# Slot projections: norm factors spread over the channels through DRAM instead of TensorE, and the order of the first loads

## The chip, the cores and the metric

The kernel runs on one core of one Trainium2 chip. The metric is device time in microseconds (us) of that core; the runs of the kernel before gave 1819.5, 1820.17 and 1820.96, median 1820.17. The engines are named as in the profile: PE (TensorE matmul; PEld its weight loads), DVE (VectorE), ACT (ScalarE), POOL (GpSimd), SP (SyncE, here only a queue that issues DMAs). PSUM is the accumulator memory that PE writes, SBUF the 128-partition on-chip memory.

## The reference

x is a float32 picture of 512 x 512 points (i, j) with 64 channels. Two layers add to it:

```
x = x + L0(gn(x))         # gn: normalize over the picture, per pair of channels (32 groups)
x = x + L1(gn(x))
```

L0 normalizes each point over its 64 channels, `xn = ln(gn(x))`, and makes two gated projections, masked by a vector m of 512 zeros and ones:

```
left  = (xn @ left_w  + left_b)  * m_i m_j * sigmoid(xn @ lgate_w + lgate_b)
right = (xn @ right_w + right_b) * m_i m_j * sigmoid(xn @ rgate_w + rgate_b)
out   = ln(einsum('kjd,kid->ijd', left, right)) @ out_w + out_b
L0    = out * sigmoid(xn @ ogate_w + ogate_b)
```

L1 keeps the first 12 x 12 Fourier modes of the picture, mixes their channels with complex weights and transforms back. All arithmetic is float32.

## The kernel before, in words

Only points whose row and column both have mask 1 give anything to the einsum. So the kernel first ranks the 512 positions (those with mask 1 first) and, if at most 256 have mask 1, works on 256 "slots" (K = 256) in place of 512 positions. The trace shows this path, `compact`.

*Ranks (lines 59 to 132).* The mask and a few constant tables are loaded by DMA; four loads of the mask, then few_i, c_tri, c_ones, c_iota and c_table go out on SP's queue, c_ident, c_center and the other constants on ACT's. DVE casts the mask into c_table (L95), two matmuls count (cum_ps), and DVE makes rank_p. Then hot, a 512 x 512 table of zeros and ones that says which position has which rank, is made by four DVE instructions of 128x512 (L116). For each of four blocks of 128 ranks four matmuls (L120) turn it into slot_t, and DVE makes src_i from it, the list of addresses for the gathers (L126). slot_row is the same as a row, read into registers by ACT and POOL.

*Gathers (lines 640 to 700).* For each of 16 column chunks jc, POOL issues four indirect DMAs of 1 MB (L632), which fetch x's rows in the order of the ranks. PE transposes the tiles, DVE takes statistics for the group norm (L681, L682), ACT copies 22 and POOL 10 of the chunk's columns to the slots of xc (L667), in turn. xc holds 128 partitions x 257 slots x 2 halves r x 64 channels: half r, partition p is the row of rank r*128+p. At the end `group_norm_affine` makes ab1, the scale and shift per channel, by a chain of small DVE instructions with two matmuls (mean_ps, var_ps).

*Slot projections (lines 703 to 789): the place of the change.* The 256 column slots are taken in 64 groups q of four. The loop's order is written out by hand (`manual_schedule`): each engine runs its instructions in the order of the program, and iteration q works on several groups at once. For one group, in order of its stages:

- `channels`: four transposes (xc_ps) put 2 x 64 channels on the partitions and 512 points on the free axis; ACT applies the affine of the group norm and writes gc_t, one of 12 buffers.
- `centered`: four matmuls with the centring matrix (cc_ps), ACT squares (sqc), DVE sums over the channels (L781) into total, 8 numbers per partition and group; here points are on the partitions again.
- `factors`: for QB = 4 groups together nine small DVE steps make 1/sqrt(variance) (rq_out, 128x32). The steps wait in a list, three of which run in each iteration.
- `spread`: POOL copies the 8 factors of a group over 64 channels each (rbc, L736).
- `normed`: four transposes by PE bring them to the layout of gc_t (rc_ps, L742), and DVE multiplies (xnc, L744).
- `project`: two matmuls each for gates and sides (L750), ACT's sigmoid (sigc, one buffer), two DVE instructions (bias added, times sigmoid: o_c, two buffers), two stores of 256 KB on SP's queue to left_d and right_d.

The loop starts 10 iterations before the first group is projected (`range(-QB - 6, groups)`). xc_ps has two PSUM buffers, cc_ps, rc_ps, gates and sides one each.

*After that* come the 64 products of the einsum (left_raw, right_raw loaded, L835 to L857), output norm, gate, statistics and the forward transform in one long pipeline, and the last layer with the stores of the result. The change does not touch these.

Of the kernel before, what the change touches and what calls it, by code (L numbers as in the profile page):

```python
# [17 lines left out]
P = 128  # L18
N = 512
# [27 lines left out]
def conv_preact_kernel(ctx: ExitStack, tc: tile.TileContext, t: dict):  # L47
# [11 lines left out]
    for b in range(4):  # L59
        nc.sync.dma_start(mask_i32[:, b : b + 1], t["sequence_mask"][:, b * P : (b + 1) * P].rearrange("o p -> p o"))  # L60

    def load_const(name, shape):
        c = const.tile(shape, F32, name=name)
        nc.scalar.dma_start(c, t[name])
        return c

    ident = load_const("c_ident", [P, P])
    center = load_const("c_center", [P, P])
    avg_p = load_const("c_avg_p", [P, P])
    avg_c = load_const("c_avg_c", [P, P])  # L70
    avg_h = load_const("c_avg_h", [P, 2])
    pick = load_const("c_pick", [P, G])
# [7 lines left out]
    nc.sync.dma_start(few_i, t["c_iota"][:, : NJ // 2])  # L80
    n_i = const.tile([1, 1], I32, name="n_i")
    with tc.tile_pool(name="ix", bufs=1) as xp, tc.tile_pool(
# [3 lines left out]
        def load_here(name, shape):  # L86
            c = xp.tile(shape, F32, name=name)
            nc.sync.dma_start(c, t[name])
            return c

        tri = load_here("c_tri", [P, P])
        ones = load_here("c_ones", [P, P])
        iota = load_here("c_iota", [P, N])
        table = load_here("c_table", [P, 4, 2 + M2])
# [20 lines left out]
        for b in range(4):  # L115
            nc.vector.tensor_scalar(hot[:, b, :], iota, rank_p[:, b : b + 1], None, ALU.is_equal)  # L116
        for sb in range(4):
            slot_ps = xps.tile([P, 2 + M2], F32, name="slot_ps", bufs=2)
            for b in range(4):
                nc.tensor.matmul(  # L120
                    slot_ps, hot[:, b, sb * P : (sb + 1) * P], table[:, b, :], start=(b == 0), stop=(b == 3)
                )
            nc.vector.tensor_copy(slot_t[:, sb], slot_ps)
            base = xp.tile([P, 1], F32, name="base", bufs=2)
            nc.vector.tensor_scalar(base, slot_t[:, sb, 0:1], float(NJ), None, ALU.mult)
            nc.vector.tensor_scalar(src_i[:, sb, :], iota[:, :NJ], base, None, ALU.add)  # L126
# [489 lines left out]
    def compact(fc):  # L616
# [31 lines left out]
        with tc.tile_pool(name="xc", bufs=1) as cp:  # L648
            xc = cp.tile([P, K + 1, 2, C], F32, name="xc")
            with tc.tile_pool(name="f1", bufs=1) as sp, tc.tile_pool(name="f1x", bufs=2) as xp, tc.tile_pool(  # L650
# [43 lines left out]
                ab1 = group_norm_affine(fc, sets, 2 * stats.shape[2], "xc")  # L694


            with tc.tile_pool(name="fb", bufs=QB + 8) as gp, tc.tile_pool(name="fw", bufs=2) as wk, tc.tile_pool(
# [7 lines left out]
                gts, totals, rss, rbs, xns, todo = {}, {}, {}, {}, {}, []  # L705

                def channels(q):
                    tps = pt.tile([P, 4, P], F32, name="xc_ps")
                    for i in range(4):
                        nc.tensor.transpose(tps[:, i, :], xc[:, 4 * q + i].rearrange("p r c -> p (r c)"), ident)  # L710
                    gts[q] = gp.tile([P, N], F32, name="gc_t")
                    nc.scalar.activation(
                        gts[q], tps.rearrange("p i k -> p (i k)"), AF.Identity, bias=ab1[:, 1:2], scale=ab1[:, 0:1]
                    )

                def centered(q):
                    cps = pc.tile([P, 8, C], F32, name="cc_ps")
                    for i in range(4):
                        nc.tensor.matmul(
                            cps[:, 2 * i : 2 * i + 2, :], gts[q][:, i * P : (i + 1) * P], center, start=True, stop=True  # L720
                        )
# [7 lines left out]
                def factors(k):  # L729
                    rss[k], steps = rsqrt_steps(rp, totals.pop(k), 1.0 / C, EPS, [P, QB * 8])  # L730
                    todo.extend(steps)

                def spread(q):
                    k, n = divmod(q, QB)
                    rbs[q] = rp.tile([P, 8, C], F32, name="rbc")
                    nc.gpsimd.tensor_copy(rbs[q], rss[k][:, 8 * n : 8 * n + 8].unsqueeze(2).to_broadcast([P, 8, C]))  # L736

                def normed(q):
                    rps = pc.tile([P, N], F32, name="rc_ps")
                    flat = rbs.pop(q).rearrange("p (i r) c -> p i (r c)", r=2)  # L740
                    for i in range(4):
                        nc.tensor.transpose(rps[:, i * P : (i + 1) * P], flat[:, i, :], ident)  # L742
                    xns[q] = wk.tile([P, N], F32, name="xnc")
                    nc.vector.tensor_mul(xns[q], gts.pop(q), rps)  # L744
# [9 lines left out]
                for q in range(-QB - 6, groups):  # L754
# [10 lines left out]
                    if live(2):  # L765
                        spread(q + 2)
                    if live(QB + 6):
                        channels(q + QB + 6)
                    if live(QB + 5):
                        sq, total = centered(q + QB + 5)  # L770
# [9 lines left out]
                    if live(QB + 5):  # L780
                        nc.vector.tensor_reduce(total, sq, AX.X, ALU.add)  # L781
                        if (q + QB + 5) % QB == QB - 1:
                            factors((q + QB + 5) // QB)
# [674 lines left out]
```

## Time and profile before

| | us |
|---|---|
| median of the runs | 1820.17 (1819.5 to 1820.96) |
| the profiled execution | 1827.94 |
| its span | 1826.1 |
| PE busy | 1643.6 (90%) |
| DVE busy | 1422.8 (78%) |
| ACT busy | 961.5 (53%) |
| POOL busy | 945.0 (52%) |

Stages by their first and last instructions in the trace: first gather issued at 14.24; last statistics of the gathers done at about 202; first gates of the slot projections at 227.24; last store of left_d issued at 466.24; first load of left_raw at 469.54.

How to read the lines. A timeline line is start, busy time, engine, source line, operation, output<-inputs, shapes, count; in brackets how long the engine idled before and what ended that. SPq and ACTq are DMA issues on these queues. Several instructions of one kind that follow each other stand in one line (a float32 matmul counts as two). PEclk is the share of full clock that PE was granted. DMA share is the mean busy share of the core's 16 DMA engines.

### The profile page before, as it was taken

How to read it: one execution, taken by the hardware profiler on the slowest of the kernel's cores; microseconds unless marked ns; L12 is line 12 of the kernel's file. 1: busy time of each engine (PE TensorE's matmuls, PEld its weight loads, DVE VectorE, ACT ScalarE, POOL GpSimd, SP SyncE). 2: the span in 40 equal slices, each digit the busy share in tenths (PEclk: the TensorE clock that was granted, in tenths of full speed). 3: DMA queues.
4: the chain of work that ended last, by engine and by line, in shares of the span. 5: the costliest groups of instructions: out<-in, count | busy, mean ns of one | idle time of the engine just before them, and what ended most of it. 6: DMA issues, size and time to landing. Idle time of an engine off the chain costs nothing. (4 is left out here: it accounts for less than half of the span.)

```text
span 1826.1 us, 33612 instructions
## 1 busy us (share of the span) xinstructions
PE 1643.6 (90%) x11414; PEld 1290.0 (71%) x11414; DVE 1422.8 (78%) x2968; ACT 961.5 (53%) x1708; POOL 945.0 (52%) x711
## 2 busy tenths in 40 slices
PE   6779899999899999998999999999999967998772
PEld 5666666665687878897888888888888844665431
DVE  6989777777555547888999999999999996765542
ACT  3565565554222249986777777777777751111000
POOL 3656211111000005788999999999999892211120
PEclk9989899999899999999999999999999986555555
DMA  6999245555655512576866776777668689999999
GB/s 253 386 385 370 102 124 137 137 138 149 203 184 175 183 58 117 197 275 237 274 238 243 258 254 229 252 268 271 241 228 291 218 251 414 423 427 426 427 427 382
DMA packets 189573, 467.94 MB, mean 256 GB/s; under 512 B 34896, under 2 KB 134224, under 8 KB 148432
## 3 DMA queue, kind: packets, MB, share of 16 engines
q1 hardware_dynamic: 158496, 262.21, 42.4%
q0 software_dynamic: 27712, 201.40, 28.7%
q10 hardware_dynamic: 3184, 2.08, 0.4%
q8 instruction: 93, 1.52, 0.3%
q14 instruction: 88, 0.72, 0.1%
HBM read 278.05 MB, written 187.56 MB: 255 GB/s over the span
## 5 line engine op out<-in xcount | busy, mean ns | idle before, releaser
L982 PE MATMUL w_ps<-gate_x,xt_c 128*128 128x128 f32 x2048 | 280.6, 281 | 30.3 <-DVE z_t L1198 24.8
L1045 POOL TENSOR_TENSOR places<-places,z_t 128x1024 f32<-128x1024 f32 x127 | 301.0, 2370 | 8.0
L982 PEld LDWEIGHTS w_ps<-gate_x,xt_c 128*128 128x128 f32 x2048 | 252.5, 194 | 45.5 <-DVE z_t L1198 40.5
L982 PE MATMUL c_ps<-center_x,xt_c 128*128 128x128 f32 x2048 | 277.4, 279 | 1.3 <-ACT xt_c L1011 0.7
L982 PEld LDWEIGHTS c_ps<-center_x,xt_c 128*128 128x128 f32 x2048 | 253.6, 195 | 4.0 <-ACT xt_c L977 2.1
L1364 PE MATMUL l_ps<-places,rinv 24*128 24x512 f32 x512 | 207.8, 1125 | 28.5 <-DVE places L1371 18.5
L1100 DVE BATCH_NORM_STATS2 stats2c<-places 128x6 f32<-128x128 f32 x1024 | 220.6, 279 | 8.0 <-POOL places L1045 8.0
L1015 DVE TENSOR_REDUCE scratch<-sq_c 128x16 f32<-128x1024 f32 x160 | 194.6, 1216 | 29.6 <-ACT sq_c L1010 18.6
L1202 POOL TENSOR_TENSOR z_t<-z_t,bias_row_out 128x1024 f32<-128x1024 f32 x32 | 75.6, 2364 | 248.5 <-DVE z_t L1198 244.4
L1149 ACT ACTIVATE z_t<-z_t 128x1024 f32<-128x1024 f32 x128 | 135.4, 1058 | 129.1 <-DVE z_t L1204 111.5
L972 PE MATMUL t_ps<-c_ident,places 128*128 128x128 f32 x1280 | 200.4, 280 | 1.3 <-DVE places L857 1.3
L1364 PEld LDWEIGHTS l_ps<-places,rinv 24*128 24x128 f32 x512 | 120.5, 303 | 110.9 <-DVE places L1371 57.2
L972 PEld LDWEIGHTS t_ps<-c_ident,places 128*128 128x128 f32 x1280 | 145.7, 142 | 61.6 <-issue 53.9
L977 ACT ACTIVATE xt_c<-t_ps,ab_xc 128x512 f32<-128x512 f32 x256 | 176.0, 688 | 14.7 <-PE t_ps L972 13.6
L1198 DVE TENSOR_TENSOR z_t<-w_ps,rs_n 128x512 f32<-128x512 f32 x256 | 172.1, 672 | 9.8 <-PE w_ps L982 9.7
L1007 ACT ACTIVATE sq_c<-c_ps 128x512 f32<-128x512 f32 x256 | 150.5, 588 | 32.8 <-PE c_ps L982 31.3
L682 DVE BATCH_NORM_STATS2 stats1c<-x_ps 128x6 f32<-128x512 f32 x256 | 156.1, 683 | 11.7 <-PE x_ps L681 11.2
L1204 DVE TENSOR_TENSOR z_t<-z_t,scratch 128x1024 f32<-128x1024 f32 x128 | 156.3, 1221 | 9.9 <-ACT rs_n L1021 3.7
L1041 POOL TENSOR_TENSOR z_t<-z_t,places 128x1024 f32<-128x1024 f32 x64 | 151.5, 2367 | 14.7 <-ACT z_t L1149 14.6
L1041 POOL TENSOR_TENSOR z_t<-z_t,bias_row_out 128x1024 f32<-128x1024 f32 x63 | 149.2, 2368 | 5.7 <-ACT z_t L1149 5.4
L1371 DVE TENSOR_TENSOR places<-places,l_ps 128x512 f32<-128x512 f32 x176 | 109.5, 683 | 54.7 <-DMA places<-x_h,dst_i 43.6
L736 POOL COPY rbc<-rq_out 128x512 f32<-128x512 f32 x64 | 38.3, 613 | 212.4 <-DVE rq_out L209 132.0
(211 smaller groups left out, 2749.1 us busy)
## 6 DMA issues: line engine op xcount, KB each, us to landing
x_h<-places SPq DMA_DIRECT2D x64, 1024.0 KB
out_x<-places SPq DMA_DIRECT2D x44, 1024.0 KB
places<-u_d SPq DMA_DIRECT2D x512, 64.0 KB
out_x<-lx_t SPq DMA_DIRECT2D x20, 1024.0 KB
left_d<-o_c SPq DMA_DIRECT2D x64, 256.0 KB
right_d<-o_c SPq DMA_DIRECT2D x64, 256.0 KB
left_raw<-left_d SPq DMA_DIRECT2D x64, 256.0 KB
right_raw<-right_d SPq DMA_DIRECT2D x64, 256.0 KB
```

The source lines that it names most:

```text
L682: nc.vector.bn_stats(stats[:, 0, 16 * (jc % quarter) + 4 * r + c, :], ps.rearrange("p i k -> p (i k)"))
L972: nc.tensor.transpose(tps[:, i, :], flat[:, o : o + P], ident)
L977: nc.scalar.activation(xts[s], tps, AF.Identity, bias=ab1[:, 2:3])
L982: nc.tensor.matmul(ps[:, 2 * i : 2 * i + 2, :], xts[s][:, i, :], w, start=True, stop=True)
L1007: nc.scalar.activation(sq, cps, AF.Square)
L1015: nc.vector.tensor_reduce(totals[k % 2][:, 8 * (n - 1) : 8 * (n + 1)], sqs.pop(s // 2), AX.X, ALU.add)
L1041: nc.gpsimd.tensor_mul(zs[k, c], zs[k, c], u)
L1045: nc.gpsimd.tensor_add(xr, xr, zs.pop((k, c)))
L1100: nc.vector.bn_stats(st[k // 4][:, g, k % 4, :], x_of(k)[:, :, 2 * g : 2 * g + 2])
L1198: nc.vector.tensor_mul(z[:, 8 * odd : 8 * odd + 8, :], wps, rs)
L1204: nc.vector.tensor_add(z, z, bias_ps["ogate"].unsqueeze(1).to_broadcast([P, 16, C]))
L1364: nc.tensor.matmul(ps.rearrange("p j o -> p (j o)"), rinv[h, b, :], it[h], start=True, stop=True, tile_position=(32 * g, 0),)
```

## The change

Four edits, all with the same arithmetic:

1. *First loads.* The mask is one DMA in place of four. c_table and c_ones move to the front of ACT's queue, ahead of c_ident and the other constants; c_tri and c_iota follow the mask on SP, few_i comes after them.
2. *Marks.* hot is made in pieces of 128 ranks: the four pieces that block 0 needs, then those of block sb+1 after the matmuls of block sb.
3. *`at_work`.* Four matmuls of 128x512 after the last transposes of the gathers and one after var_ps, whose results nobody reads.
4. *Factors.* `spread` and `normed` change. For four groups together PE transposes rq_out once (to 32 x 128), ACT copies it out of PSUM, POOL's queue writes it to a DRAM tile rs_d (16 KB), and two more DMAs on POOL's queue, one for each half r, read it back to 64 partitions each, every partition reading the same four rows of 512 numbers: rbc is 128 x 4 x 512, two buffers. DVE multiplies from rbc directly. POOL's copies and PE's four transposes per group are gone. gc_t has no buffers of its own: `channels` writes over the group's part of xc, which it has just transposed. The loop starts 14 iterations ahead (lead = QB + 9), spread comes five iterations before the group's first multiply, and total's order of columns is (r, i) in place of (i, r).

```
-    for b in range(4):
-        nc.sync.dma_start(mask_i32[:, b : b + 1], t["sequence_mask"][:, b * P : (b + 1) * P].rearrange("o p -> p o"))
+    nc.sync.dma_start(mask_i32, t["sequence_mask"].rearrange("o (b p) -> p (o b)", p=P))
...
-        tri = load_here("c_tri", [P, P])
-        ones = load_here("c_ones", [P, P])
-        iota = load_here("c_iota", [P, N])
-        table = load_here("c_table", [P, 4, 2 + M2])
+        table = load_here(nc.scalar, "c_table", [P, 4, 2 + M2])
+        tri = load_here(nc.sync, "c_tri", [P, P])
+        ones = load_here(nc.scalar, "c_ones", [P, P])
+        iota = load_here(nc.sync, "c_iota", [P, N])
+        ident = load_const("c_ident", [P, P])
...
+        nc.sync.dma_start(few_i, t["c_iota"][:, : NJ // 2])
...
-        for b in range(4):
-            nc.vector.tensor_scalar(hot[:, b, :], iota, rank_p[:, b : b + 1], None, ALU.is_equal)
+        def mark(sb):
+            for b in range(4):
+                one = slice(sb * P, (sb + 1) * P)
+                nc.vector.tensor_scalar(hot[:, b, one], iota[:, one], rank_p[:, b : b + 1], None, ALU.is_equal)
+
+        mark(0)
         for sb in range(4):
...
+            if sb < 3:
+                mark(sb + 1)
...
+                def at_work(count):
+                    ps = pt.tile([P, 4, P], F32, name="x_ps")
+                    for _ in range(count):
+                        nc.tensor.matmul(ps, ident, flat[:, : 4 * P], start=True, stop=True)
+
+                at_work(4)
+                ab1 = group_norm_affine(fc, sets, 2 * stats.shape[2], "xc", with_variance=lambda ab: at_work(1))
...
+            rs_d = dram.tile([K // 4, 2, 4 * P], F32, name="rs_d")
...
+                def gts(q):
+                    return xc[:, 4 * q : 4 * q + 4].rearrange("p i r c -> p (i r c)")
...
-                def spread(q):
-                    k, n = divmod(q, QB)
-                    rbs[q] = rp.tile([P, 8, C], F32, name="rbc")
-                    nc.gpsimd.tensor_copy(rbs[q], rss[k][:, 8 * n : 8 * n + 8].unsqueeze(2).to_broadcast([P, 8, C]))
+                def spread(k):
+                    ps = pc.tile([QB * 8, P], F32, name="rc_ps")
+                    nc.tensor.transpose(ps, rss.pop(k), ident)
+                    turned = np_.tile([QB * 8, P], F32, name="turned_c")
+                    nc.scalar.copy(turned, ps)
+                    groups_d = rs_d[k * QB : (k + 1) * QB]
+                    nc.gpsimd.dma_start(groups_d.rearrange("n r (i p) -> (n r i) p", p=P), turned)
+                    rbs[k] = np_.tile([P, QB, N], F32, name="rbc")
+                    for r in range(2):
+                        h = slice(r * C, (r + 1) * C)
+                        nc.gpsimd.dma_start(rbs[k][h], groups_d[:, r].unsqueeze(0).to_broadcast([C, QB, N]))
...
                 def normed(q):
-                    rps = pc.tile([P, N], F32, name="rc_ps")
-                    flat = rbs.pop(q).rearrange("p (i r) c -> p i (r c)", r=2)
-                    for i in range(4):
-                        nc.tensor.transpose(rps[:, i * P : (i + 1) * P], flat[:, i, :], ident)
+                    k, n = divmod(q, QB)
                     xns[q] = wk.tile([P, N], F32, name="xnc")
-                    nc.vector.tensor_mul(xns[q], gts.pop(q), rps)
+                    nc.vector.tensor_mul(xns[q], gts(q), rbs[k][:, n])
...
-                for q in range(-QB - 6, groups):
+                lead = QB + 9
+                for q in range(-lead - 1, groups):
...
-                    if live(2):
-                        spread(q + 2)
-                    if live(QB + 6):
-                        channels(q + QB + 6)
-                    if live(QB + 5):
-                        sq, total = centered(q + QB + 5)
+                    if live(lead + 1):
+                        channels(q + lead + 1)
+                    if live(lead - QB) and (q + lead - QB) % QB == QB - 1:
+                        spread((q + lead - QB) // QB)
+                    if live(lead):
+                        sq, total = centered(q + lead)
```

In the changed program the order on each engine follows: on DVE the multiply of group q+1 comes first in iteration q, then up to three rsqrt steps, then o_c of group q and the reduce of group q+13; on PE gates(q), xc_ps(q+14), every fourth time the new transpose, cc_ps(q+13), sides(q).

## The prediction

> **What bounds the kernel now.** I read the page's slices first (which stage leans on what), then a table by stretches of 50 us, then one period of the slot projections in the timeline, then the two ends of the stretch that the change touches: the first 14 us and 199 to 215 us.
>
> ```profile
> PE   6779899999899999998999999999999967998772
> ...
> PEclk9989899999899999999999999999999986555555
> DMA  6999245555655512576866776777668689999999
> ```
>
> Slices are 45.7 us. The first four (gathers) are at 9 in DMA. Slices 5 to 10 are the slot projections: PE at 8 and 9, DMA at 4 and 5.
>
> ```profile
> core 0: us, PE busy (x) PEld busy (x) DVE busy (x) ACT busy (x) POOL busy (x), PEclk, DMA share, GB/s
> 100.00:150.00 50.00, 40.60 (x279) 34.05 (x280) 42.84 (x83) 28.16 (x95) 30.25 (x65) 0.90 0.97 381
> ...
> 300.00:350.00 50.00, 50.00 (x314) 32.29 (x312) 38.53 (x82) 29.68 (x40) 7.80 (x13) 1.00 0.55 138
> ```
>
> In the projections PE is busy 50.00 of 50 us at full clock, DVE 77%, ACT 59%. So there a TensorE instruction taken away is time, until the next engine is full. One period:
>
> ```profile
> 268.55 1.13 PE L750 MATMUL sides_c<-xnc,w_sides 64*128 64x512 f32 x4
> ...
> 269.51 1.02 PE L750 MATMUL gates_c<-xnc,w_gates 64*128 64x512 f32 x4
> ...
> 269.78 1.41 DVE L776 SCALAR_TENSOR_TENSOR o_c<-sides_c,b_sides,sigc 128x512 f32<-128x512 f32 x2 [1.23 <-ACT sqc L723]
> ...
> 270.47 0.65 PE L742 MATMUL rc_ps<-c_ident,rbc 128*128 128x128 f32 x4
> ...
> 270.96 0.60 PE L710 MATMUL xc_ps<-c_ident,xc 128*128 128x128 f32 x4
> ...
> 271.11 0.68 DVE L781 TENSOR_REDUCE total<-sqc 128x8 f32<-128x512 f32 x1
> ...
> 271.31 1.11 ACT L759 ACTIVATE sigc<-gates_c,b_gates 128x1024 f32<-128x1024 f32 x1 [1.55 <-DVE o_c L776]
> ...
> 271.40 1.06 PE L719 MATMUL cc_ps<-c_center,gc_t 128*128 128x128 f32 x8
> ...
> 271.70 0.68 DVE L744 TENSOR_TENSOR xnc<-gc_t,rc_ps 128x512 f32<-128x512 f32 x1
> ...
> 272.32 0.77 ACT L712 ACTIVATE gc_t<-xc_ps,ab_xc 128x512 f32<-128x512 f32 x1
> ```
>
> The next sides start at 272.38: 3.83 us a period, and from start to start PE's five blocks take 0.96, 0.96, 0.49 (rc_ps), 0.44 and 0.98, without a gap.
>
> ```profile
> 4.94 0.43 SPq L88 DMA_DIRECT2D c_table<-in_c_table  x1
> 7.63 0.17 DVE L95 CAST c_table<-mask_i 128x4 f32<-128x4 int32 x1 [7.63 <-DMA c_table<-in_c_table]
> ...
> 10.82 1.68 DVE L116 TENSOR_SCALAR hot<-c_iota,rank_p 128x512 f32<-128x512 f32 x4
> ...
> 11.36 6.90 PEld L120 LDWEIGHTS slot_ps<-c_table,hot 128*128 128x128 f32 x32 [2.37 <-DVE hot L116]
> ...
> 14.24 1.08 POOL L632 DMA_INDIRECT xg<-in_x,src_i  x1 [13.78 <-DVE src_i L126]
> ```
>
> The stretches after the gathers, in the columns of the table above:
>
> ```profile
> 199.21:203.94 4.73, 0.00 (x1) 0.01 (x1) 4.53 (x12) 0.00 (x0) 2.83 (x10) 1.00 0.00 0
> 203.94:209.34 5.40, 2.98 (x13) 2.50 (x13) 3.00 (x19) 0.83 (x2) 0.00 (x0) 0.50 0.00 0
> 209.34:214.86 5.52, 5.34 (x25) 4.88 (x25) 0.71 (x2) 2.64 (x5) 0.00 (x0) 0.56 0.00 0
> ```
>
> The first gather waits for a chain that starts with c_table, the last of nine issues on SP. After the gathers PE idles 4.7 us and then runs at clock 0.50 until about 214.
>
> The profiled execution took 1827.94 us (span 1826.1), 7.8 above the median 1820.17; I sum against it and move the difference to the median.
>
> **The change, part by part.**
>
> **Ranks' chain.** c_table goes to the front of ACT's queue (issued at 0.75 as c_ident was), and the mask is one transfer at 0.76 in place of four. By c_table's own 2.69 us from issue to use (4.94 to 7.63) the table is there at 3.4. The mask moves 512 scattered elements in one transfer; I give it half a microsecond more, so the CAST starts at about 4.2 instead of 7.63: 3.4 us. c_tri (second on SP, 1.2+2.7=3.9) and c_iota (1.7+2.7=4.4, needed 3.2 after the CAST) don't end later. The first marks are 128 wide: four at 0.42 pitch become four at 0.17 (the small DVE rows of this chain) to 0.42, but the four matmuls behind them keep 0.44 each (7.03/16), so only about 0.3 is gained. The later marks sit on DVE before a slot's copy, 0.7 us of work within the 1.7 us that PE needs for a slot. Sum -3.7; from -4.6 (mask as quick as the table) to 0 (mask as late as the table was). The other constants and few_i, moved behind these, are needed after 20 us. The whole gather stage behind it moves along: its copies alternate ACT and POOL without a break and its DMA share is 0.97 wherever it starts.
>
> **at_work.** Four matmuls of 512 columns at 0.48 (half of the 0.96) fill PE from 199.2 to about 201.1, one more follows var_ps, before transposes that wait for ab anyway (done 207.95, used 208.51: 0.56 us of cover for 0.5 to 1.0). If PE then stays at full clock, the first two iterations from 209.34 take 2 x 1.85 (the later pitch, 214.86, 216.70, 218.55) instead of 5.52: -1.8; if not, 0 to +0.4. The row shows only that 4.7 us of idling ends at clock 0.50; the longest gap left is 2.8. I take -1.8, since 2.8 is well short of 4.7; by the row alone it could be either. The Trainium skill, "TensorE: Matmul & The Clock Gate" (The HAM clock gate), says the clock is halved after an idle window of about 3.4 us; by it a gap of 2.8 us leaves the clock up, -1.8, and one of 4.7 us does not.
>
> **Longer lead.** The loop starts 14 iterations ahead instead of 10: 4 x 1.85 = +7.4 before the first gates, while PE does nothing else. The same channel work ends four iterations earlier at the end: four iterations fall from 3.83 to the bare pitch of the tail (2.79, from 452.43, 455.21, 458.00): -4.2.
>
> **Factors.** Out of PE: four transposes, 0.49 a period. In: one transpose of a 32-column piece per four groups, 0.12/4=0.03. Period 3.37; x50 iterations with all the work: 50 x 0.46 = -23.0. Covered beside it: DVE (0.68+0.68+1.41 and three short steps at 0.21; start to start 3.16, under 3.37), with the multiply now reading SBUF twice, for which I keep 0.68 and bound 0.59 to 0.75; ACT (1.11+0.77+0.60, and 0.3 of copy in one of four). POOL loses its copies (0.61) and gets three DMA issues per four groups; nothing else waits on POOL in this stage. gc_t is now written into xc itself, with PE and ACT waiting only as they did.
>
> **DMA.** Stores move 134 GB/s at share 0.53, so 253 GB/s when full, 2.0 us of all engines per period. Per four groups come 16 KB written and two loads of 512 KB. At 393 GB/s (gathers, 381/0.97) the loads cost 2.7 us, at the stores' 253 (also 64 partitions at a time) 4.1; the worst row of this trace, the first loads (100 GB/s at 0.60, 4 to 6 us), makes 6.3. I take 4.1: 8.1+4.1=12.2 of 13.5 us, share 0.9.
>
> **The new wait.** The multiply of a fourth group waits for the loads; behind it on DVE stand the rsqrt steps, o_c and the reduce, and PE's gates wait for it. spread's copy ends about 3.8 us into its iteration (sigmoid to 2.7, gc to 3.5), the multiply comes 5 iterations and 2.2 us after that iteration's start: 5 x 3.37+2.2-3.9 = 15.1 us for write, loads and both issues. One gather of 1 MB took from 14.24 to its first use at 21.16, 6.9 us, 4.2 of them fixed: write 4.2 + loads 6.9 = 11.1 on idle engines, and up to two periods' stores (4.0) in between: 15.1. So it just fits, and I price it at 0 in the steady part. In the lead an iteration is 1.85, which leaves 4 x 1.85+1.9 = 9.3: the first multiply waits 1.8 (0 to 5).
> o_c has two buffers: a store must land within 2 x 3.37-1.4-0.5 = 4.8 us of the second issue (5.8 before). In the tail it lands within 3.65 (issue 450.02, buffer reused 453.67), once 5.0. Sharing engines with a load may add 1.0 (half of 2.0): 4.65. I put +4 for stalls (0 to +17).
> The Trainium skill, "DMA: Bandwidth & Descriptors" (Queues, rings and completion order), speaks against the change here: an engine drains a whole packet of some 9 to 17 descriptors from one queue before it turns to the next. By it a load (16 rows of 2 KB on each engine) would go first in one piece, 2.1 us, the store would land at 5.7, and 0.9 lost twice in each of some 12 groups would make +21 and leave almost no gain; no row here shows it.
>
> Sum: -3.7 -1.8 +7.4 +1.8 -23.0 -4.2 +4 = -19.5: 1808.4 for the profiled execution, 1800.7 for the median.
>
> **Rivals.**
> A, transfers bind: the loads cost 6.3 us a group (all partitions read the same few rows of DRAM, which no row shows). Period (8.1+6.3)/4=3.6: 50 x 0.23 = -11.5 in place of -23+4: 1820.2-3.7-1.8+7.4+1.8-11.5-4.2 = 1808. For it: share 0.9 already. Against: the gathers run at 0.97 without harm.
> B, slower: write, then loads, take more than the lead covers. Each microsecond over 15.1 costs 1/5.6 per iteration, 50/5.6 = 8.9 us in all; from 17.7 us on (23.5 lost) the change is no gain. At 19 us: +34.8-23.5 = +11.3, 1831. For it: two dependent trips through DRAM stand where POOL copied in 0.61 us, and 11.1 is for idle engines. Against: even with stores between it is 15.1.
> C, the change doesn't do what it says: PE stays at 3.83 because DVE or the sigmoid's buffer fills the gap. Then only the rest counts: -3.7-1.8+7.4+1.8-4.2 = -0.5, 1819.7, no change. Against: the tail turns at 2.79 with the same sigmoid and o_c.
>
> **How the numbers follow.** Forecast 0.60 (its own range 1793 to 1806), A 0.22 (of it 0.04 within 0.2%, where stalls come on top), B 0.15, C 0.03. 0.2% is 3.6 us, about what can be told from no change here (three runs span 1.5). So faster 0.60+0.18=0.78, same 0.04+0.03=0.07, slower 0.15. The low end 1791 is the forecast without stalls or first wait and with -4.6 for the ranks (-26.2, 1794) and 3 for DVE and ACT copies I may have overcharged; the high end 1824 leaves B out, with its 0.15.
>
> **What would show it.** Right: the first gather at about 10.5 us; clock 1.00 through 204 to 215; the first gates about 2 to 3 us later than 227.24; a period of 3.37 at PE 50 of 50; DMA share 0.85 to 0.9; left_d's last store about 19 us earlier. Wrong: DVE's multiply waiting on DMA rbc every fourth group (B), o_c waiting on DMA left_d or right_d (A, or packets), a pitch over 3.6, clock 0.50 after 204.

## The result, and the profile after

The changed kernel takes 1840.51 us (1838.37 to 1844.18), the kernel before on the same chip 1820.57: ratio 1.0108, 95% interval 1.0096 to 1.012. It is about 20 us slower, where the prediction had 19.5 us faster. The prediction was wrong.

The two ends of the change went as forecast, or better. The first lines of the timeline after (start, duration, engine, line, operation; in brackets the idle time before and what ended it):

```profile
3.29 0.17 DVE L93 CAST c_table<-mask_i 128x4 f32<-128x4 int32 x1 [3.29 <-DMA mask_i<-in_sequence_mask]
...
9.86 1.09 POOL L637 DMA_INDIRECT xg<-in_x,src_i  x1 [9.40 <-DVE hot L117]
```

The cast now waits for the mask, at 3.29 instead of 7.63 us, and the first gather leaves at 9.86 instead of 14.24: 4.4 us earlier. The stretches after the gathers and the middle of the slot projections, in the columns of the table by stretches (busy us of PE, PEld, DVE, ACT, POOL, then PE's granted clock, DMA share, GB/s):

```profile
196.00:200.00 4.00, 2.55 (x9) 1.01 (x7) 2.77 (x17) 0.00 (x0) 1.19 (x4) 1.00 0.00 0
200.00:204.00 4.00, 3.79 (x18) 2.96 (x18) 1.60 (x10) 1.55 (x2) 0.00 (x0) 0.57 0.00 0
204.00:208.00 4.00, 3.44 (x29) 2.97 (x28) 1.38 (x2) 2.61 (x5) 0.00 (x0) 1.00 0.00 0
...
300.00:350.00 50.00, 44.87 (x247) 26.16 (x248) 37.54 (x79) 28.97 (x41) 5.27 (x9) 0.97 0.71 192
```

The clock is back at 1.00 at 204 us. But PE, which had been busy 50.00 of 50 us in the middle, is busy only 44.87, and the DMA engines, at 0.71, aren't full either. So something new makes both wait. The waits of DVE in the whole stage (total us, times, longest) name it:

```profile
DVE o_c L801 <- DMA right_d<-o_c: 38.0, 14, 5.1
...
DVE xnc L768 <- DMA rbc<-rs_d: 1.3, 1, 1.3
```

The multiply by the factors (xnc) waits for its loads once, for 1.3 us, at the start; the long way through DRAM is covered. What waits is o_c, the result of a group, for the store of an earlier group out of the same buffer: 14 times, 38.0 us. Before, this wait came once, for 1.2 us. One of the 14 in the timeline:

```profile
256.98 1.23 POOL L761 DMA_DIRECT2D rbc<-rs_d  x2 [1.66 <-DVE rq_y L205]
257.59 1.41 DVE L801 SCALAR_TENSOR_TENSOR o_c<-sides_c,b_sides,sigc 128x512 f32<-128x512 f32 x2 [0.60 <-PE sides_c L774]
259.02 0.45 SPq L813 DMA_DIRECT2D left_d<-o_c  x1
259.51 0.64 SPq L813 DMA_DIRECT2D right_d<-o_c  x1
261.00 1.41 DVE L801 SCALAR_TENSOR_TENSOR o_c<-sides_c,b_sides,sigc 128x512 f32<-128x512 f32 x2 [0.26 <-PE sides_c L774]
...
266.94 1.41 DVE L801 SCALAR_TENSOR_TENSOR o_c<-sides_c,b_sides,sigc 128x512 f32<-128x512 f32 x2 [2.79 <-DMA right_d<-o_c]
```

Two loads of 512 KB are issued from 256.98 on. The stores issued at 259.02 and 259.51 come out of the buffer filled at 257.59; that buffer is wanted again two iterations later and is free only at 266.94, 7.4 us after right_d's issue. What the 16 DMA engines did meanwhile, by queue, in four stretches one after the other (258 to 258.5, 259 to 261.5, 261.5 to 263.5 and 263.5 to 265 us; q1 carries the stores, q0 GpSimd's transfers; packets, MB, share of all engines):

```profile
q1 hardware_dynamic: 45, 0.17, 98.8%
...
q0 software_dynamic: 111, 0.43, 94.5%
...
q0 software_dynamic: 112, 0.40, 70.2%
q1 hardware_dynamic: 52, 0.18, 22.1%
...
q1 hardware_dynamic: 98, 0.34, 68.6%
q0 software_dynamic: 53, 0.17, 31.6%
```

From 259 to 261.5 us the queue of the stores moved nothing at all, with two stores issued. In that time the loads moved 0.43 MB. Not all of this is delay, since a store alone needs a time to start too. In the tail of the kernel before, on engines with nothing else to do, the pair of stores issued at 449.53 and 450.02 moved nothing up to 450.5 us; all its bytes went between 450.5 and 452.8:

```profile
q1 hardware_dynamic: 151, 0.52, 90.3%
```

So a pair alone starts 1.1 us after left_d's issue and needs 2.2 us from its first bytes to its last. In the change the first bytes go between 261.8 and 262.0, 2.8 us after the issue, and from them to the free buffer it takes another 5.1 us, in which the queues share the engines, at first with the larger part for the loads. (The next pair, issued at 262.43, is among it already: from 261.8 to 267 us the stores move 1.02 MB.) The store stands still for 1.7 us longer than it would alone, and then goes at reduced speed, which costs 2.9 us.

Where the 14.4 us by which the last right_d store is later (481.07 against 466.73 us) come from, in stages of the two profiled executions: first gather -4.4; from there to the first centring multiply 192.75 instead of 195.10 us, -2.35; from there to the first gates 25.25 instead of 17.90, +7.35; from the first gates to the last store 253.21 instead of 239.49, +13.7. The loss is all in the steady stage. Without stalls I had forecast -27.2 for it; of the 40.9 us between that and +13.7, 38.0 are waits for right_d.

The stalls cost clock too. In this stage PE's granted clock fell to 0.50 five times, four times for 3.4 us and once for 6.8, where before it stayed at 1.00 from 230 to 460 us. Each fall lies in or up to 3 us behind one of the five longest waits for right_d (3.4 to 5.1 us, ended at 299.42, 347.27, 379.09, 444.25 and 461.52); the nine others, of at most 2.8 us, have none. A stretch of the first fall:

```profile
302.50:305.50 3.00, 3.00 (x11) 1.52 (x8) 2.77 (x7) 2.21 (x5) 0.70 (x2) 0.50 0.80 195
```

Other waits grow with it: o_c waits for sides_c for 17.8 us in all, against 4.0 in the run with four buffers below; its waits for the factors' copy on ACT (turned_c) are 3.7 us against 12.3. So the loss isn't the 38.0 us alone; longer and shorter waits beside it nearly cancel.

(The spans of the two executions differ by 10.5 us only, and the medians by 19.9: behind the last store the profiled execution of before took 1359.4 us and that of the change 1355.5, and the first is 7.8 above its median, the second 2.1 below.)

### The profile page after: what moved, and what is told of

It reads as the page before. It is cut to its first block, busy times and chain, and to the rows that moved or that the text cites. A ratio compares the mean times of both kernels' runs of the same rounds, so it can differ in the third digit from the quotient of the medians.

```text
span 1836.6 us, 33095 instructions
## 1 busy us (share of the span) xinstructions
PE 1621.4 (88%) x11184; PEld 1258.2 (69%) x11184; DVE 1425.9 (78%) x2980; ACT 964.6 (53%) x1724; POOL 936.3 (51%) x695
## 5 line engine op out<-in xcount | busy, mean ns | idle before, releaser
L1391 PE MATMUL l_ps<-places,rinv 24*128 24x512 f32 x512 | 207.3, 1107 | 30.3 <-DVE places L1398 19.5
L1068 POOL TENSOR_TENSOR z_t<-z_t,places 128x1024 f32<-128x1024 f32 x64 | 151.6, 2369 | 13.8 <-ACT z_t L1176 13.7
L801 DVE SCALAR_TENSOR_TENSOR o_c<-sides_c,b_sides,sigc 128x512 f32<-128x512 f32 x128 | 90.2, 746 | 70.6 <-DMA right_d<-o_c 38.0
```

The costliest lines, as they stand in the source:

```text
L1068: nc.gpsimd.tensor_mul(zs[k, c], zs[k, c], u)
L1391: nc.tensor.matmul(ps.rearrange("p j o -> p (j o)"), rinv[h, b, :], it[h], start=True, stop=True, tile_position=(32 * g, 0),)
```

## The experiments

Theory: the loads delay the stores, and o_c has too few buffers to bear the delay. Rivals: the loads as a whole fill the engines (A), the chain through DRAM (B), or some other cost of the new scheme. The ratios are against the kernel before on the chip of each run.

**One part alone: the first loads, marks and PE's five multiplies, with the factors spread as before.**

```diff
-                def spread(k):
...
+                def spread(q):
+                    k, n = divmod(q, QB)
+                    rbs[q] = rp.tile([P, 8, C], F32, name="rbc")
+                    nc.gpsimd.tensor_copy(rbs[q], rss[k][:, 8 * n : 8 * n + 8].unsqueeze(2).to_broadcast([P, 8, C]))
...
-                lead = QB + 9
-                for q in range(-lead - 1, groups):
+                for q in range(-QB - 6, groups):
```

> The first loads, the marks and at_work as in the changed kernel, the factors and the lead as before. The slot projections then have their old period of 3.83 us. In the changed kernel's trace the first gather goes out 4.4 us earlier and the first full-clock iteration saves 1.8 to 2.1. Theory (all of the loss sits in the factors' way through DRAM): 6 to 7 us under the kernel before, about 1814. Rival (part of the loss is a different start of the gathers or of later stages): no gain or a loss.

Measured: 1815.28 us, ratio 0.9959 (0.9946 to 0.9972), so 5 to 10 us faster. The head of the change is a gain of the size forecast, and the whole loss lies in the factors' part.

**No loads after the first group of four.** The same tile of factors serves all slots, so the right scaling of the later slots is left out.

```diff
+                    if k > 0:
+                        rbs[k] = rbs[0]
+                        return
-                    rbs[k] = np_.tile([P, QB, N], F32, name="rbc")
+                    rbs[k] = np_.tile([P, QB, N], F32, name="rbc", bufs=1)
```

> The changed kernel without the 30 loads after the first two: all groups are multiplied by the factors of the first 16 slots, which leaves out the right scaling of the others. The transposes, copies and writes to DRAM stay. Theory (the loads are the whole loss): the period is 3.37 to 3.41 in all iterations with no wait for right_d, and the last left_d store goes out 24 to 27 us earlier than before the change; 1793 to 1800. Rival (DVE or the order of the engines holds the period as well): the period stays over 3.6.

Measured: 1800.66 us, ratio 0.9881 (0.9862 to 0.9901). The wait for right_d falls to 0.8 us in all. Taking the loads away gives some 40 us: what PE, DVE and ACT do in the new scheme is as cheap as forecast.

**Four buffers for o_c.** All loads stay.

```diff
-            ) as rp, tc.tile_pool(name="fg", bufs=1) as sp, tc.tile_pool(name="fo", bufs=2) as op, tc.tile_pool(
+            ) as rp, tc.tile_pool(name="fg", bufs=1) as sp, tc.tile_pool(name="fo", bufs=4) as op, tc.tile_pool(
```

> The changed kernel with four o_c buffers instead of two. Theory (a store waits behind the loads' packets, and o_c has no buffer free until it lands): the waits of o_c for right_d, 38 us in the changed kernel, fall under 8 us, a group of four takes about 13.7 us instead of 15.8, and the time falls by 25 to 33 us, to 1808 to 1815. Rival (the loads are too slow in themselves, so that loads and stores together fill the DMA engines): a group stays at 15 us or more, the DMA share in the projections rises to 0.95, and at most 10 us are gained. Rival (the multiply waits for the loads): waits of xnc on rbc appear, which the changed kernel has only once.

Measured: 1801.4 us, ratio 0.9884 (0.9864 to 0.9905), the same as with no loads. The stretch of 300 to 350 us and the queues from 270 to 274.5 us of this run, in the columns of before:

```profile
300.00:350.00 50.00, 50.00 (x300) 30.88 (x300) 43.33 (x90) 33.30 (x47) 5.79 (x10) 1.00 0.85 239
```

```profile
q0 software_dynamic: 249, 0.95, 83.0%
q1 hardware_dynamic: 12, 0.02, 1.6%
```

PE is full again, DMA share 0.85. The second view shows that the stores are delayed as much as before the edit, or more: in 4.5 us they moved 0.02 MB against the loads' 0.95 MB, with stores issued at 270.04, 270.53, 273.47 and 273.96. The first bytes of the pair of 270.04 go 3.9 us after the issue. Nobody waits for them: no wait for right_d is left in the stage. The delay costs only where the buffer is wanted. That also rules out that the loads fill the engines (A): all the bytes move, at the same total, without loss. What does come back is a little of B: the multiply waits for its loads four times, 4.4 us in all, the longest 2.7 us at 428.85.

**Three buffers.**

```diff
-            ) as rp, tc.tile_pool(name="fg", bufs=1) as sp, tc.tile_pool(name="fo", bufs=2) as op, tc.tile_pool(
+            ) as rp, tc.tile_pool(name="fg", bufs=1) as sp, tc.tile_pool(name="fo", bufs=3) as op, tc.tile_pool(
```

> The change with one edit: three buffers for o_c instead of two. Theory (a store lands up to 3.75 us too late for two buffers, once in four iterations): a third buffer gives one iteration, 3.4 us, of cover, which leaves at most 0.35 us a group, 5 us in all: 1801 to 1807 us. Rival (the stores queue up behind each other, so that the delay grows with the buffers): waits of over 1 us a group stay, 1810 to 1830 us.

Measured: 1805.62 us, ratio 0.9905 (0.9876 to 0.9934).

```profile
DVE o_c L801 <- DMA right_d<-o_c: 7.6, 4, 3.0
```

The time is within what was expected, but not for the reason given: I had allowed for at most 0.35 us in each group, and there are four waits, the longest of 3.0 us. The 0.35 took every stall for at most 3.75 us; in the change two waits were longer, 5.1 and 4.8 us, both in the last iterations (at 444.25 and 461.52), and the two longest waits here, 2.3 and 3.0 us, lie late as well (418.45 and 432.54). There an iteration takes 2.8 us and not 3.4, so a third buffer covers less.

**Four buffers in the kernel before.** The control: do more buffers help in any case?

```diff
-            ) as rp, tc.tile_pool(name="fg", bufs=1) as sp, tc.tile_pool(name="fo", bufs=2) as op, tc.tile_pool(
+            ) as rp, tc.tile_pool(name="fg", bufs=1) as sp, tc.tile_pool(name="fo", bufs=4) as op, tc.tile_pool(
```

> The kernel before with one edit: four buffers for o_c instead of two. Theory (its steady iterations never wait for a store, and TensorE sets 3.83 us an iteration): 1817 to 1825 us, no change that shows. Rival (more buffers help in any case, and the gain of the four buffers in the changed kernel is not that of the stall): 1810 us or lower.

Measured: ratio 0.9995 (0.9981 to 1.0009), no difference. So four buffers are no gain in themselves; in the changed kernel they gain by the stall that they take away.

**The two loads of a group two iterations apart.**

```diff
-                    for r in range(2):
-                        h = slice(r * C, (r + 1) * C)
-                        nc.gpsimd.dma_start(
-                            rbs[k][h], groups_d[:, r].unsqueeze(0).to_broadcast([C, QB, N])
-                        )
+                    load(k, 0)
+                def load(k, r, queue=nc.gpsimd):
+                    h = slice(r * C, (r + 1) * C)
+                    queue.dma_start(rbs[k][h], rs_d[k * QB : (k + 1) * QB, r].unsqueeze(0).to_broadcast([C, QB, N]))
...
                         spread((q + lead - QB) // QB)
+                    if live(lead - QB - 2) and (q + lead - QB - 2) % QB == QB - 1:
+                        load((q + lead - QB - 2) // QB, 1)
```

> The change with one edit: of the two loads of a group of four, the second (right half of the channels) is issued two iterations after the first, so that a burst is 512 KB and not 1 MB; bytes, buffers and queue stay. Theory (a store waits behind the burst that is in flight): a burst takes half of the 4.6 us of all engines that a group's loads took, so a store lands at about 3.65 + 2.3 = 5.0 to 6.0 us after right_d's issue instead of 7.4, and o_c waits 0 to 1.2 us, twice in four iterations, instead of 2.5 to 3.75 once: 1802 to 1820 us. Rival (what counts is the load traffic as a whole, however it is cut): stalls of the same sum, 1835 to 1845 us.

Measured: 1840.61 us, ratio 1.0104 (1.0066 to 1.0141): not what the theory expected. The timeline tells why:

```profile
258.30 1.23 POOL L763 DMA_DIRECT2D rbc<-rs_d  x2 [1.66 <-DVE rq_w L207]
```

Both loads still leave together. In the program they stand two iterations apart, but GpSimd has nothing else to do or to wait for in these iterations, so it runs ahead. The edit changed nothing in time, and says nothing on the length of a burst.

**Both loads on ScalarE's queue, one iteration after the write.**

```diff
-                    for r in range(2):
-                        h = slice(r * C, (r + 1) * C)
-                        nc.gpsimd.dma_start(
-                            rbs[k][h], groups_d[:, r].unsqueeze(0).to_broadcast([C, QB, N])
-                        )
+                def load(k, r, queue=nc.gpsimd):
+                    h = slice(r * C, (r + 1) * C)
+                    queue.dma_start(rbs[k][h], rs_d[k * QB : (k + 1) * QB, r].unsqueeze(0).to_broadcast([C, QB, N]))
...
+                    if live(lead - QB - 1) and (q + lead - QB - 1) % QB == QB - 1:
+                        for r in range(2):
+                            load((q + lead - QB - 1) // QB, r, nc.scalar)
```

> The change with one edit: both loads of a group are issued on ScalarE's queue, one iteration after the write (which stays on GpSimd's queue). Theory (any burst on another queue delays the stores on SyncE's queue): o_c waits on right_d as before the edit, 2 to 4 us in each group, 1835 to 1845 us, and up to 14 us more if ScalarE's two issues of some 0.6 us per group fall on the path. Rival (it is GpSimd's queue, whose descriptors software writes, that holds the engines): no waits on right_d, 1800 to 1808 us.

Measured: 1835.88 us, ratio 1.0078 (1.0048 to 1.0108). The queues from 259.5 to 262 us (q10 now carries the loads; stores issued at 259.98 and 260.47):

```profile
q10 hardware_dynamic: 237, 0.47, 81.8%
q1 hardware_dynamic: 10, 0.00, 0.2%
```

The first bytes of the pair go between 262.25 and 262.5 us, 2.3 us after its issue instead of 1.1, and o_c waits for right_d 11 times, 29.6 us. So it isn't something of GpSimd's queue alone: large loads on ScalarE's queue do it too.

**Loads of 64 distinct rows.** The loads read x instead of the factors, so the right scaling is left out.

```diff
                         nc.gpsimd.dma_start(
-                            rbs[k][h], groups_d[:, r].unsqueeze(0).to_broadcast([C, QB, N])
+                            rbs[k][h],
+                            x[0, h].rearrange("h w c -> h (w c)")[:, k * QB * N : (k + 1) * QB * N].rearrange("h (n c) -> h n c", n=QB),
                         )
```

> The change with one edit: the two loads read 64 distinct rows of 8 KB of the input x each, where the change reads one row of 8 KB 64 times; sizes, queue and buffers stay, and the loads no longer wait for the write. It leaves out the right factors: the scaling of the slots is by numbers of x. Theory (a burst of 1 MB delays the store, wherever it comes from): loads land in 7 to 8 us, o_c waits on right_d 2 to 4 us in each group, 1834 to 1845 us. Rival (64 readings of the same row are what makes the loads slow): loads land below 5.5 us, waits below 1 us a group, 1801 to 1815 us.

Measured: 1838.95 us, ratio 1.0093 (1.0063 to 1.0123), 12 waits for right_d of 33.7 us together. The queues from 257 to 261 us:

```profile
q0 software_dynamic: 125, 0.89, 99.8%
```

Now the loads move 0.22 MB/us while they have the engines for themselves, against 0.43/2.5 = 0.17 in the change, and land in 6.1 us in the median instead of 7.5. The edit changes two things, though: 64 distinct rows instead of one row 64 times, and pieces of 8 KB in a row of DRAM instead of 2 KB (7.1 KB a packet in the mean here, 0.43 MB in 111 packets or 3.9 KB in the change). Which of them makes the fourth or so of the speed, this run doesn't tell. The stores issued at 258.50 and 258.99 move nothing up to 261.25, when the loads have all but moved their megabyte, and the time of the kernel is the same within its uncertainty: where the bytes come from isn't the cause.

**Loads of 256 KB, one in each iteration, on ScalarE's queue.** ScalarE does work by iterations, so that these really lie apart (issued at 256.64, 261.77, 263.15, 266.96 and 270.38 in the trace).

```diff
-                    for r in range(2):
-                        h = slice(r * C, (r + 1) * C)
-                        nc.gpsimd.dma_start(
-                            rbs[k][h], groups_d[:, r].unsqueeze(0).to_broadcast([C, QB, N])
-                        )
+                def load(k, s, r, queue):
+                    h = slice(r * C, (r + 1) * C)
+                    two = slice(2 * s, 2 * s + 2)
+                    queue.dma_start(
+                        rbs[k][h, two], rs_d[k * QB + 2 * s : k * QB + 2 * s + 2, r].unsqueeze(0).to_broadcast([C, 2, N])
+                    )
...
+                    for part in range(4):
+                        at = q + lead - QB - 1 - part
+                        if 0 <= at < groups and at % QB == QB - 1:
+                            load(at // QB, part // 2, part % 2, nc.scalar)
```

> Against the run with both loads on ScalarE's queue (1835.9 us): the same queue and the same bytes, but each group's loads cut into four of 256 KB (two groups of slots, one half of the channels), one in each of four iterations; ScalarE works iteration by iteration, so here the issues really lie apart, which the two loads on GpSimd's queue, two iterations apart in the program, did not. Theory (while a load drains, the stores get nothing: 2.8 us for 512 KB by the bytes per half microsecond, so 1.4 us for 256 KB): a store lands at 3.65 + 1.4 = 5.1 us after its issue, 0.3 us past the 4.8 that two buffers cover; stalls of at most 0.3 us in each of some 56 iterations, 0 to 17 us over the floor: 1801 to 1818 us, the middle 1808. Rival (loads anywhere cost their bytes, however they are cut): waits on right_d of some 20 us in the middle of the stage as with two loads, 1832 to 1840 us.

Measured: 1811.92 us, ratio 0.992 (0.9896 to 0.9943).

```profile
DVE o_c L807 <- DMA right_d<-o_c: 12.1, 14, 1.8
```

Same bytes, same queue, two buffers: with the burst cut and spread, the ratio goes from 1.0078 to 0.992, some 29 us, and the waits from 29.6 to 12.1 us. What counts is how the bytes are cut and spread, not how many they are. A little remains, 0.9 us a wait.

**Loads of 128 KB, each group's own, on GpSimd's queue.** In the program each group's two loads stand in an iteration of their own, with six buffers.

```diff
-                    rbs[k] = np_.tile([P, QB, N], F32, name="rbc")
+                def load_factors(q):
+                    rbs[q] = np_.tile([P, N], F32, name="rbc", bufs=6)
                     for r in range(2):
                         h = slice(r * C, (r + 1) * C)
-                        nc.gpsimd.dma_start(
-                            rbs[k][h], groups_d[:, r].unsqueeze(0).to_broadcast([C, QB, N])
-                        )
+                        nc.gpsimd.dma_start(rbs[q][h], rs_d[q, r].unsqueeze(0).to_broadcast([C, N]))
...
-                    nc.vector.tensor_mul(xns[q], gts(q), rbs[k][:, n])
+                    nc.vector.tensor_mul(xns[q], gts(q), rbs.pop(q))
...
+                    if live(5):
+                        load_factors(q + 5)
```

> The changed kernel with two buffers for o_c, but each group of four slots gets its own two loads of 128 KB in its own iteration (four iterations ahead of their use) instead of two loads of 512 KB once in four. The same bytes, in short bursts. Theory (the length of one burst delays a store): a load of 128 KB on 16 engines takes about 0.5 us, two take 1.1, a store lands within 4.8 us of its issue, the waits for right_d go, and the period is 3.4 to 3.5 in every iteration: 1808 to 1815. Rival (bytes, not bursts): a period of 3.8 to 4.0 as in the changed kernel, only spread evenly; 1835 to 1845.

Measured: 1805.3 us, ratio 0.9895 (0.9873 to 0.9916). The waits for right_d did not go, as the theory had it, but fell to 14.2 us in 12 times. And the loads were not paced by iterations:

```profile
264.37 1.03 POOL L763 DMA_DIRECT2D rbc<-rs_d  x2
266.35 3.09 POOL L763 DMA_DIRECT2D rbc<-rs_d  x6 [0.95 <-DVE rq_v L204]
```

After each write GpSimd issues the two loads of one group and, a little later, those of three more, 0.51 us each, and then waits some 8 us for the next write. So here too the megabyte goes out once in four iterations, within 5.1 us instead of 1.2. That the waits fall all the same comes from the smaller loads or from this slower issue; the runs don't separate the two.

**The same with four buffers for o_c.**

```diff
-            ) as rp, tc.tile_pool(name="fg", bufs=1) as sp, tc.tile_pool(name="fo", bufs=2) as op, tc.tile_pool(
+            ) as rp, tc.tile_pool(name="fg", bufs=1) as sp, tc.tile_pool(name="fo", bufs=4) as op, tc.tile_pool(
```

> Two edits of the change together: each group of slots has its own two loads of 128 KB with six buffers, issued iteration by iteration, and o_c has four buffers. Theory (the store stall is the only loss, and each edit removes most of it): no waits on right_d, and nothing more to gain than without any loads, which gave 1800.7 us: 1798 to 1803 us. Rival (128 issues on GpSimd instead of 32 hold up the factors' steps on the same engine): 1803 to 1810 us.

Measured: 1801.14 us beside 1826.29 of the kernel before on that chip, ratio 0.9862 (0.9839 to 0.9885); PE busy 50.00 of 50 us, no wait for right_d. The loads leave as in the run before, eight in about 5 us. It and the one-number edit to four buffers can't be told apart; both are faster than the kernel before, by 1.4% and 1.2%.

**Four buffers, without the five multiplies that keep PE at work.**

```diff
-                at_work(4)
-                ab1 = group_norm_affine(fc, sets, 2 * stats.shape[2], "xc", with_variance=lambda ab: at_work(1))
+                ab1 = group_norm_affine(fc, sets, 2 * stats.shape[2], "xc")
```

> The change with four buffers for o_c (1801.4 us), and without the five multiplies that keep TensorE at work over the norm's statistics. Theory (they were put at 1.8 us of the sum): 1802 to 1805 us. Rival (the clock falls in that gap with and without them, since the changed kernel still shows 0.57 between 200 and 204 us): 1800 to 1802 us. Rival (without them the first sixteen groups run at half clock, as before, for some 7 us): 1806 to 1810 us.

Measured: ratio 0.9892 (0.9866 to 0.9917), against 0.9884 with them: inconclusive in time. The clock shows a difference (196 to 216 us of this run):

```profile
196.00:200.00 4.00, 0.00 (x0) 0.00 (x0) 3.90 (x10) 0.00 (x0) 1.78 (x6) 0.80 0.02 4
...
208.00:216.00 8.00, 7.50 (x45) 6.50 (x44) 2.66 (x4) 5.24 (x8) 0.00 (x0) 0.74 0.00 0
```

Half clock lasts from 198.4 to 212.1 us here, and from 199.4 to 202.8 in the run with the multiplies. There the first gates came at 227.13, here at 232.46 us, but 2.9 of these 5.3 us were left at the last store (443.28 and 446.16), and the spans of the two executions are 1800.6 and 1800.7.

## Why the prediction was wrong

The step that failed is the one on o_c's two buffers: "Sharing engines with a load may add 1.0 (half of 2.0): 4.65. I put +4 for stalls (0 to +17)." It has two errors. The first is what a load adds to a store. The 3.65 that it starts from was only an upper bound, the time until the buffer was used again (o_c at 453.67 waited for PE there, not for a store); the bytes of that pair had moved 2.8 us after right_d's issue. The stall shown took 7.4 us, so the loads added 4.6 us where 1.0 was priced: 1.7 us of standing still, which the step doesn't have at all since it lets the store *share* the engines from its first byte on, and 2.9 us in the sharing itself. The 7.4 us are far past the 4.8 that two buffers cover. The second is the bound of 17, too low for a wait of 2.7 us in the mean at 14 places. The term measured 37.1 us: from first gates to last store 253.21 us in the change, 216.15 with four buffers.

The terms of the sum, each in the stretch where it was to show:

| step | forecast, us | measured, us |
|---|---|---|
| ranks' chain (to the first gather) | -3.7 | -4.4 |
| first gather to first centring multiply | 0 | -2.35 |
| PE kept at work, longer lead and first wait (from there to the first gates) | -1.8 +7.4 +1.8 | +7.35, 1.3 of it the wait |
| steady iterations and tail, without stalls | -23.0 -4.2 | -23.3 (with four buffers) |
| store stalls | +4 | +37.1 |
| sum at the last store | -19.5 | +14.4 |

- Ranks' chain: the transposed mask landed as early as the table, at 3.29, not half a microsecond later.
- First gather to first centring multiply: no term had this gain of 2.35 us. In the eleven runs with the five multiplies the stretch took 190.3 to 195.8 us, against 195.10 before, so a part of it at least can be the spread between executions.
- PE at work: the forecast was that a longest gap of 2.8 us leaves the clock up. The gaps were shorter still, 1.0 us between mean_ps and var_ps, and the clock did fall to 0.50, at 200.0 us; it rose after 3.4 us instead of the 10 of before, so that little of the dip was left behind the first centring multiply (202.61), where the -1.8 was to be gained. In the run with the head alone, where the clock did not fall, this stretch took 16.06 us (202.04 to 218.12) with the old lead, 1.8 less than the 17.90 of before. The Trainium skill, "TensorE: Matmul & The Clock Gate" (The HAM clock gate), as I had used it, asks for an idle window of some 3.4 us; here a window in which PE was idle for part of the time was enough.
- Lead: the three terms of this stretch came to 7.35 of 7.4. The first gates came at 227.86, 0.6 us later than before; the sum makes 3.7, and the 2 to 3 of the prediction's last paragraph does not follow from it. The difference is the 2.35 above and the 0.7 of the ranks' chain.
- Steady period: with the stalls gone, 18 starts of o_c from 230.94 to 289.13 us are 3.42 us apart, where I had 3.37. Every fourth iteration, in which o_c waits for the factors' transpose and its copy (0.9 us "<-ACT turned_c" in these), takes 3.47 to 3.52 us, the others 3.37 to 3.44. Over 50 iterations the 0.05 is 2.5 of the 3.9 us that are missing; the waits for the loads from 404 us on (3.3 us) are another part. In the tail nothing changed, 2.78.
- The write and the loads: the chain of 15.1 us did fit in the change, and rival B fell: one wait of 1.3 us. With four buffers, where nothing else held the iterations up, it just fits: four waits, 4.4 us. The loads took 28.7% of the engines over 210 us (230 to 440 us; 14.3 MB, 13.7 groups), 4.4 us a group; 4.1 were priced.
- Rival A took the loads as bytes that fill the engines. The share was 0.71, and with four buffers 0.85 at no loss: it is not the cause. Rival C fell: the period does go to 3.4.
- The Trainium skill, "DMA: Bandwidth & Descriptors" (Queues, rings and completion order), says that an engine goes through a whole packet of one queue before it turns to the next. The row of the queues agrees in kind: nothing for the stores, then a share. My estimate by it was +21 and "almost no gain"; that was too little. In the stall shown the loads moved 0.53 MB ahead of the store, about the one load of the estimate, but in 3.2 us (258.6 to 261.8) instead of 2.1, and what the sharing cost afterwards was not in it. I set it aside because no row showed it; no row had shown equal sharing either. The two ends of the range should have held both.

The stall is what turned a gain into a loss. That four buffers give 1801.4 us, beside the 1800.7 of the forecast, is in part luck all the same: the forecast held +4 for stalls that are gone there, and in that run a first stretch 3.5 us shorter than before (191.61 us), in no term, makes up for the 3.9 us that the steady part is short.

What isn't settled: by what unit the engines change from one queue to the other. Before a store's first bytes the loads moved 0.53 MB in the stall shown, some 1 MB with distinct rows, and 0.82 MB between 270 and 273.75 us with four buffers. No run here varied that alone. Nor do the runs tell whether smaller loads help by their size or by being issued more slowly.

## What to carry to other kernels

Before a large load is put beside a stream of stores, ask not only whether the engines have room in the mean (0.71 to 0.85 here) but how long one store may be late: the buffer must bear a store that stands still behind a load and is slow afterwards (7.4 us here instead of 2.8). Where it can't, one or two more output buffers (here one number, 1840 to 1801 us) cure it, and the same bytes in smaller loads cure most of it (ratio 0.992 and 0.9895). An instruction on an engine that waits for nothing is not paced by standing in a later iteration of the program: neither the two loads of 512 KB nor those of 128 KB on GpSimd's queue were.

## What the runs showed of the hardware that I had not expected

- Stores behind large loads on another queue, GpSimd's or ScalarE's, moved their first bytes 2.8, 2.3 and 3.9 us after the issue in the three stalls shown (the change, ScalarE's loads, four buffers), against 1.1 us alone; in the change from 259 to 261.5 us they moved nothing and the loads 0.43 MB.
- Loads in which 64 partitions read the same rows, in pieces of 2 KB, went at 0.17 MB/us, of 64 distinct rows of 8 KB at 0.22; both held nearly all engines (94.5% and 99.8%).
- PE's clock fell to 0.50 after a stretch in which the longest idle gap was about 1 us. With the same five multiplies in all of them, one execution of each, it didn't fall there at all in four runs (the head alone, no loads, three buffers, ScalarE's loads), for 3 to 4 us in five (the change among them) and for 7 us in two. So these executions don't show a fixed length of the dip for the same instructions.
- Long waits for an output buffer brought half clock on PE with them: in the change those of 3.4 us and more and none of 2.8 or less, with three buffers also those of 2.3 and 3.0 us (0.50 from about 420.9 and 434.5 us on).
